# Gathers that leave item 0 out by a bounds check, in place of products that subtract it

## The chip, the cores and the metric

The kernel runs on one core of a Trainium2 chip, launched once with all its inputs in device memory. The metric is device time in microseconds (us). A time given for a kernel is the median of its runs; a profile is one more execution, in which the hardware profiler records each instruction, and that execution has a time of its own. Engines are called PE (TensorE, matrix products and transposes), DVE (VectorE), ACT (ScalarE), POOL (GpSimd) and SP (SyncE, which only issues transfers here).

## The reference

The inputs are a sequence of 50 item indices for each of 1024 users, a length per user, and a table of 100,001 items with 128 numbers each. Item 0 is a padding item: its row counts as zero, both where rows are gathered and in the product at the end.

```python
emb = emb_table.at[0].set(0.0)
e = emb[seq]                                   # 1024 x 50 x 128
prefix = jnp.cumsum(e, axis=1)
denom = jnp.minimum(t_idx[None, :], lengths[:, None])
uF = prefix / denom[:, :, None]
mean = uF.mean(axis=0)
var = uF.var(axis=0)
y = (uF - mean) * lax.rsqrt(var + BN_EPS) * gamma + beta
def step(v, x):                                # 50 steps
    v = v + (x - v) / TAU
    spike = atan_spike(v - V_TH)               # 1 where v >= V_TH
    v = v - spike * V_TH
    return (v, spike)
scores = spikes.mean(axis=0) @ emb.T           # 1024 x 100001
```

The scores are 1024 x 100,001 numbers of four bytes, 409.6 MB. The indices of the run are drawn evenly from 0 (in the first column from 159) up to between 90,260 and 99,965, so that an index 0 is rare: 1024 x 50 draws from some 100,000 values.

## The kernel before, in words

The kernel has two stages. In the first, a loop over the 50 steps t, the running sums are kept transposed, with the 128 features on the partitions and the 1024 users along the free axis, in two banks `pre[0]` and `pre[1]` of 512 users in PE's accumulator memory. In the second, the spike counts are multiplied with the whole table, and the scores are written out.

The order of the work is written out by hand (`tc.manual_schedule()`): each engine executes its instructions in the order in which the program names it, and only semaphores tie the engines together.

**The first stage.** `gather(t)` (L204) takes one of two buffers `e` (128 partitions x 1024 numbers, a pool with `bufs=2`) and has POOL issue eight indirect transfers (L207), one for each group of 128 users; each reads 128 indices from column t of the tile `idx` and fetches 128 rows of 512 bytes from the table. Gathers 0 and 1 are issued ahead of the loop; gather t + 2 is issued in step t, after PE has read buffer e_t. In step t PE transposes the eight blocks of e_t and adds them to `pre` (L324). DVE divides each half by the length into `uF` (L335) and takes its statistics (L336), which L342 joins to mean and variance. ACT takes a square root (L346) and subtracts the mean (L353); four small operations of DVE (L359 to L372) make the scale `a`; ACT applies it and writes the input x into the tile of v (L376, in the function `x`). DVE counts the spikes of the step before (L301), and adds the old state (L379, in `step`). ACT then computes v minus the threshold in bf16 (L294, in `over`), from which DVE makes the negative rest state in the next step (L298).

**Item 0.** The table as given does not have zeros in row 0, and the gathers fetch that row as it is. The kernel before subtracts it by products. At the start it makes `isz`, 1 where an index is 0 (L219 to L221), transposes it into `zT` (L224, L226), which has one row for each step and user, and splits row 0 of the table into a high and a low part, negated, in `r0n` (L227 to L232). `only(t)` (L267) builds, for five steps at a time, a matrix that is `r0n` where the row belongs to step t and zero elsewhere (L272), by means of `sel` (L234). `correct(t, l)` (L280) multiplies it with `zT` into both halves of `pre` (L282), which takes row 0 away from every user whose index is 0 in step t. Step t issues the correction of step t + 1, and the correction of step 0, with `start=True`, is what opens the accumulation. Row 0 of the table for the product at the end is set to zero separately (L133), which the change does not touch.

Beside the steps, SP fetches the first forty 1024-row blocks of the table (L109) at the start, and in steps 42 and 44 the first two are transposed (L136) and split into two parts for the product (L152 on ACT, L153 on DVE).

**The second stage** goes over 98 blocks of the table and eight groups of 128 users: products of both parts (L160), a scaled copy of the result by DVE or ACT (L512, L514), and the store of the scores (L169 on SP). The change does not touch it.

Of the kernel before, what the change touches and what calls it, by code (L numbers as in the profile page):

```python
# [12 lines left out]
F32 = mybir.dt.float32  # L13
BF16 = mybir.dt.bfloat16
F32R = mybir.dt.float32r
I32 = mybir.dt.int32
U32 = mybir.dt.uint32
AF = mybir.ActivationFunctionType
ALU = mybir.AluOpType

P = 128
# [4 lines left out]
BANK = 512  # L26
GROUP = 6
AHEAD = 6
ONLY = 5
TWICE = 2  # L30
ASIDE = 2
SHIFT = TWICE + ASIDE
# [7 lines left out]
def rec_kernel(  # L40
# [9 lines left out]
    nc = tc.nc  # L50
    B, T = seq.shape
    N, D = table.shape
    NB = B // P
# [21 lines left out]
    ident = const.tile([P, P], F32, tag="ident", name="ident")  # L75
# [11 lines left out]
    def pair(i):  # L87
        free.append([embp.tile([P, HALF], F32R, tag=f"{x}{i}", name=f"{x}_{i}") for x in ("hi", "lo")])
# [59 lines left out]
    def prepare(q, pt):  # L148
        turned(q, pt)
        split[q] = hi, lo = free.pop(0)  # L150
        vp, vh, vl = views(q, pt, hi, lo)
        nc.scalar.copy(vh, vp)  # L152
        nc.vector.tensor_tensor(vl, vp, vh.bitcast(F32), ALU.subtract)  # L153
# [18 lines left out]
    with ExitStack() as ph:  # L172
        once = ph.enter_context(tc.tile_pool(name="once", bufs=1))
        lp = ph.enter_context(tc.tile_pool(name="lif", bufs=1))
        sp = ph.enter_context(tc.tile_pool(name="stats", bufs=3))
        up = ph.enter_context(tc.tile_pool(name="uF", bufs=1))
        gp = ph.enter_context(tc.tile_pool(name="gather", bufs=2))
        accp = ph.enter_context(tc.tile_pool(name="acc", bufs=1, space=bass.MemoryType.PSUM))
        vp = ph.enter_context(tc.tile_pool(name="v", bufs=1, space=bass.MemoryType.PSUM))

        idx = once.tile([P, NB, T], I32, tag="idx", name="idx")
        nc.sync.dma_start(out=idx, in_=seq.rearrange("(p n) t -> p n t", n=NB))
        len_i = once.tile([P, NB], I32, tag="len_i", name="len_i")
        nc.sync.dma_start(out=len_i, in_=lengths.rearrange("(p n) -> p n", n=NB))
        r0 = once.tile([P, D], F32, tag="r0", name="r0")
        nc.sync.dma_start(out=r0, in_=table[0:1, :].to_broadcast([P, D]))
        gb = once.tile([P, 2], F32, tag="gb", name="gb")
        nc.sync.dma_start(out=gb[:, 0:1], in_=gamma.rearrange("(d o) -> d o", o=1))
        nc.sync.dma_start(out=gb[:, 1:2], in_=beta.rearrange("(d o) -> d o", o=1))
# [9 lines left out]

        es = {}

        def gather(t):  # L204
            es[t] = gp.tile([P, B], F32, tag="e", name=f"e_{t}")
            for n in range(NB):
                nc.gpsimd.indirect_dma_start(  # L207
                    out=es[t][:, n * P : (n + 1) * P],
                    out_offset=None,
                    in_=table,  # L210
                    in_offset=bass.IndirectOffsetOnAxis(ap=idx[:, n, t : t + 1].bitcast(U32), axis=0),
                )

        make_identity(nc, ident)
        isz = up.tile([P, NB, P], F32, tag="uF", name="isz")
        rb = up.tile([P, NB, P], F32, tag="uF", name="rb")
        gather(0)

        nc.vector.memset(isz, 0.0)  # L219
        for u in (0, P // 2):  # L220
            nc.vector.tensor_single_scalar(isz[:, :, u : u + T], idx, 0.0, ALU.is_equal)  # L221
        zps = vp.tile([P, B], F32, tag="v1", name="zps")
        for n in range(NB):
            nc.tensor.transpose(zps[:, n * P : (n + 1) * P], isz[:, n, :], ident)  # L224
        zT = once.tile([P, B], F32R, tag="zT", name="zT")
        nc.scalar.copy(zT, zps)  # L226
        r0hi = once.tile([P, D], F32R, tag="r0hi", name="r0hi")  # L227
        nc.scalar.copy(r0hi, r0)
        r0n = once.tile([P, D], F32, tag="r0n", name="r0n")
        nc.vector.tensor_scalar_mul(r0n, r0hi.bitcast(F32), -1.0)  # L230
        up2 = slice(P // 2, P)
        nc.vector.tensor_tensor(r0n[up2, :], r0hi[up2, :].bitcast(F32), r0[up2, :], ALU.subtract)  # L232
        sel = once.tile([P, P // 2], F32, tag="sel", name="sel")
        nc.vector.tensor_tensor(sel, ident[:, : P // 2], ident[:, P // 2 :], ALU.add)  # L234


        rl = once.tile([P, NB], F32, tag="rl", name="rl")
        nc.vector.tensor_copy(rl, len_i)
# [17 lines left out]
        count = once.tile([P, B], BF16, tag="count", name="count")  # L256
# [5 lines left out]

        pre = [accp.tile([P, BANK], F32, tag=f"pre{h}", name=f"pre{h}") for h in range(B // BANK)]

        ls = once.tile([P, ONLY, D], F32R, tag="ls", name="ls")

        def only(t):  # L267

            k = t % ONLY
            if k == 0:  # L270
                n = min(ONLY, T - t)
                nc.vector.tensor_tensor(  # L272
                    ls[:, :n, :],
                    r0n.unsqueeze(1).to_broadcast([P, n, D]),
                    sel[:, t : t + n].unsqueeze(2).to_broadcast([P, n, D]),
                    ALU.mult,
                )
            return ls[:, k, :]

        def correct(t, l):  # L280
            for h in range(B // BANK):
                nc.tensor.matmul(  # L282
                    pre[h],
                    lhsT=l,
                    rhs=zT[:, h * BANK : (h + 1) * BANK],
                    start=t == 0,
                    stop=False,
                    skip_group_check=True,
                )

        def over(t, v):

            d = lp.tile([P, B], BF16, tag="d", name=f"d_{t}")
            nc.scalar.activation(d, v, AF.Identity, bias=less)  # L294
            return d
# [4 lines left out]
        def spiked(out, cs, v):  # L300
            nc.vector.scalar_tensor_tensor(out, v, V_TH, count[:, cs], ALU.is_ge, ALU.add)  # L301
# [9 lines left out]

        v = None

        correct(0, only(0))
        l = only(1)
        gather(1)
        for t in range(T):
            last = t == T - 1
            e = es.pop(t)
            uF = up.tile([P, B], F32, tag="uF", name=f"uF_{t}")  # L320
            bs = sp.tile([P, B // BANK, 6], F32, tag="bs", name=f"bs_{t}")
            for h, cs in enumerate(halves):
                for k in range(0, BANK, P):
                    nc.tensor.matmul(  # L324
                        pre[h][:, k : k + P],
                        lhsT=e[:, h * BANK + k : h * BANK + k + P],
                        rhs=ident,
                        start=False,
                        stop=last,
                        is_transpose=True,  # L330
                        skip_group_check=True,
# [2 lines left out]
                        keep_busy(ident, KQ // 2)  # L334
                nc.vector.scalar_tensor_tensor(uF[:, cs], rlen[:, cs], 1.0 / (t + 1), pre[h], ALU.max, ALU.mult)  # L335
                nc.vector.bn_stats(bs[:, h, :], uF[:, cs])  # L336
            if t + 2 < T:
                gather(t + 2)
            if not last:
                correct(t + 1, l)  # L340
            mv = sp.tile([P, 2], F32, tag="mv", name=f"mv_{t}")
            nc.vector.bn_aggr(mv, bs.rearrange("p h s -> p (h s)"))  # L342

# [31 lines left out]
            def x(vt, cs):  # L375
                nc.scalar.activation(vt, uF[:, cs], AF.Identity, bias=hgb[:, 1:2], scale=a)  # L376

            def step(vt, cs):
                nc.vector.scalar_tensor_tensor(vt, negv[:, cs], -0.5, vt, ALU.mult, ALU.add)  # L379

            if not last:
                vt = vp.tile([P, B], F32, tag=f"v{(t + 1) % 2}", name=f"v_{t}")
                x(vt, whole)
                if t:
                    spiked(count, whole, v)
                step(vt, whole)
                v = vt
                if t == T - 2:
                    spiked(count, whole, v)
                    moved = once.tile([P, P], F32, tag="r0hi", name="moved")  # L390
                    nc.vector.tensor_scalar_add(moved, v[:, pieceA], beta2)
                    near = once.tile([P, P], F32, tag="r0", name="near")
                    nc.vector.scalar_tensor_tensor(near, v[:, pieceA], V_TH, moved, ALU.is_ge, ALU.subtract)
                d = over(t, v)
                if t + 2 < T:
                    l = only(t + 2)

                if t in (T - 8, T - 6):
                    q = (t - T + 8) // 2
                    pair(q)  # L400
                    prepare(q, vp.tile([P, HALF], F32, tag="v0", name=f"pt_{q}"))
                    if q == TWICE - 1:
                        for k in range(TWICE):
                            rows[GROUP + ASIDE + k] = first[:, k, :]
                        nc.sync.dma_start(
                            out=first[:, :TWICE, :],
                            in_=table[(GROUP + ASIDE) * HALF : (GROUP + SHIFT) * HALF, :].rearrange(
                                "(q p k) d -> p q (k d)", p=P, k=KQ
                            ),
                        )  # L410
# [53 lines left out]
    for c, W in enumerate(WIDTHS):  # L464
# [34 lines left out]
        for n in range(NB):  # L499
            if c == 0 and n == 0:  # L500
                continue
            pool, tag, most = turns[blocks % len(turns)]
# [23 lines left out]
            if n in (1, 4) and c >= MIDDLE and to_fetch < parts:  # L526
                g, k = divmod(to_fetch - SHIFT, GROUP)
# [26 lines left out]
```

## Time and profile before

| | |
|---|---|
| Time, median of 3 runs | 1573.99 us (1573.79 to 1574.6) |
| The profiled execution's own time | 1638.64 us |
| Its span, first to last instruction | 1636.8 us |
| Busy in the span: PE, DVE, ACT, POOL | 1085.8, 948.7, 673.0, 381.1 us |
| POOL's gathers: first and last start | 3.4 and 564.2 us |
| First store of scores issued | 577.6 us |
| Written to memory, read from memory | 409.6 MB, 77.7 MB |

A page of the profile has the busy time of each engine, the span in 40 equal slices of 40.9 us (a digit is the busy share of a slice in tenths), the queues of transfers, the chain of waits that ended last, and groups of instructions by source line. In a group's line stand the line, engine, operation, output and inputs with their shapes, the count, the busy time and the mean of one in ns, and the engine's idle time just before these instructions with what ended it. "issue" is time in which an engine waited for nothing that the profile shows; "remote" is a release whose source is not in the records.

### The profile page before, as it was taken

How to read it: one execution, taken by the hardware profiler on the slowest of the kernel's cores; microseconds unless marked ns; L12 is line 12 of the kernel's file. 1: busy time of each engine (PE TensorE's matmuls, PEld its weight loads, DVE VectorE, ACT ScalarE, POOL GpSimd, SP SyncE). 2: the span in 40 equal slices, each digit the busy share in tenths (PEclk: the TensorE clock that was granted, in tenths of full speed). 3: DMA queues.
4: the chain of work that ended last, by engine and by line, in shares of the span. 5: the costliest groups of instructions: out<-in, count | busy, mean ns of one | idle time of the engine just before them, and what ended most of it. 6: DMA issues, size and time to landing. Idle time of an engine off the chain costs nothing.

```text
span 1636.8 us, 12254 instructions
## 1 busy us (share of the span) xinstructions
PE 1085.8 (66%) x4464; PEld 806.9 (49%) x4464; DVE 948.7 (58%) x1127; ACT 673.0 (41%) x697; POOL 381.1 (23%) x406
## 2 busy tenths in 40 slices
PE   4333332333332488888988877888878888788884
PEld 2212111222112366666766666666666666566663
DVE  5666654677665865665755554555545555555652
ACT  2333322333323354555554444444444444444442
POOL 7666666766666500000000000000000000000000
PEclk7555555555555599999999999989999999999998
DMA  9611111111111279999999999999999999999998
GB/s 346 240 46 46 46 45 46 51 45 47 45 46 47 66 326 412 415 423 412 405 426 430 427 428 429 403 432 426 418 428 420 408 423 426 427 424 408 429 401 358
DMA packets 51313, 488.12 MB, mean 298 GB/s; under 512 B 10079, under 2 KB 10336, under 8 KB 30004
## 3 DMA queue, kind: packets, MB, share of 16 engines
q1 hardware_dynamic: 30752, 430.86, 62.6%
q0 software_dynamic: 12800, 26.24, 5.4%
q10 hardware_dynamic: 7700, 30.23, 4.5%
q8 instruction: 35, 0.57, 0.1%
q14 instruction: 26, 0.21, 0.0%
HBM read 77.69 MB, written 409.60 MB: 298 GB/s over the span
## 4 chain that ended last, share of the span: by engine, by line
DMA 42%; PE 16%; DVE 14%; another core or an unknown queue 9%; POOL 7%; issue 5%; ACT 5%; ACTq 0%; SPq 0%; DVEq 0%; POOLq 0%
DMA scores<-o 40%; PE po L160 14%; POOL e L207 7%; DVE o L512 3%; ACT o L514 3%; DVE uF L335 2%; DVE bs L336 2%; DMA e<-in_L_rec_emb_table,idx 2%; DVE v L379 2%; DVE negv L298 1%; ACT v L376 1%; PE pre L324 1%; DVE count L301 1%; DVE pairs L153 1%
## 5 line engine op out<-in xcount | busy, mean ns | idle before, releaser
L512 DVE TENSOR_SCALAR o<-po 128x1024 f32<-128x1024 f32 (+1 forms) x391 | 467.4, 1214 | 326.0 <-DMA scores<-o 183.8
L514 ACT ACTIVATE o<-po 128x1024 f32<-128x1024 f32 x391 | 391.8, 1025 | 503.9 <-DMA scores<-o 358.6
L207 POOL DMA_INDIRECT e<-in_L_rec_emb_table,idx x400 | 380.4, 951 | 183.5 <-issue 110.9
L160 PE MATMUL po<-pairs,countB 128*128 128x512 f32 (+1 forms) x1120 | 291.2, 406 | 61.1 <-ACT o L514 61.1
L160 PE MATMUL po<-pairs,countC 128*128 128x512 f32 (+1 forms) x840 | 237.8, 430 | 59.0 <-ACT o L514 53.1
L160 PEld LDWEIGHTS po<-pairs,countB 128*128 128x128 f32 x1120 | 210.4, 193 | 122.0 <-ACT o L514 80.0
L282 PE MATMUL pre<-zT,ls 128*128 128x512 f32 x100 | 78.4, 786 | 271.2 <-DVE uF L335 227.2
L160 PEld LDWEIGHTS po<-pairs,countC 128*128 128x128 f32 x840 | 166.2, 205 | 111.0 <-ACT o L514 65.0
L282 PEld LDWEIGHTS pre<-zT,ls 128*128 128x128 f32 x100 | 29.0, 291 | 309.9 <-DVE uF L335 255.7
L324 PE MATMUL pre<-ident,e 128*128 128x128 f32 x400 | 126.8, 435 | 79.5 <-DMA e<-in_L_rec_emb_table,idx 63.0
L335 DVE SCALAR_TENSOR_TENSOR uF<-rlen,pre 128x512 f32<-128x512 f32 x100 | 68.0, 680 | 161.7 <-remote 124.4
L324 PEld LDWEIGHTS pre<-ident,e 128*128 128x128 f32 x400 | 80.4, 209 | 126.8 <-DMA e<-in_L_rec_emb_table,idx 94.7
L153 DVE TENSOR_TENSOR pairs<-pt,pairs 128x1024 fp32r<-128x1024 f32 x70 | 85.3, 1218 | 96.1 <-ACT pairs L152 96.0
L346 ACT ACTIVATE r<-mv,eps 128x1 f32<-128x1 f32 x50 | 14.8, 295 | 273.0 <-DVE mv L342 181.0
L136 PE MATMUL pt<-ident,rows 128*128 128x128 f32 (+1 forms) x768 | 105.6, 283 | 9.9 <-issue 4.9
L136 PEld LDWEIGHTS pt<-ident,rows 128*128 128x128 f32 (+1 forms) x768 | 95.1, 148 | 27.4 <-issue 11.5
L160 PE MATMUL po<-hi,countB 128*128 128x512 f32 x208 | 85.4, 411 | 13.9 <-ACT o L514 13.6
L152 ACT CAST pairs<-pt 128x1024 fp32r<-128x1024 f32 x70 | 70.1, 1013 | 41.0 <-PE pt L136 41.0
L160 PE MATMUL po<-lo,countB 128*128 128x512 f32 x208 | 83.2, 400 | 0.0
L294 ACT ACTIVATE d<-v,less 128x1024 bf16<-128x1024 f32 x49 | 54.5, 1113 | 65.4 <-DVE v L379 36.3
L160 PE MATMUL po<-hi,countC 128*128 128x512 f32 x156 | 66.5, 426 | 14.2 <-ACT o L514 12.6
L376 ACT ACTIVATE v<-uF,hgb,a 128x1024 f32<-128x1024 f32 x49 | 59.2, 1208 | 31.0 <-DVE a L372 11.7
(88 smaller groups left out, 887.2 us busy)
## 6 DMA issues: line engine op xcount, KB each, us to landing
scores<-o SPq DMA_DIRECT2D x96, 3072.0 KB
scores<-o SPq DMA_DIRECT2D x32, 1536.0 KB
scores<-o SPq DMA_DIRECT2D x30, 1024.0 KB
rows<-in_L_rec_emb_table ACTq DMA_DIRECT2D x19, 1536.0 KB
scores<-o SPq DMA_DIRECT2D x8, 2896.5 KB
rows<-in_L_rec_emb_table SPq DMA_DIRECT2D x5, 3072.0 KB
e<-in_L_rec_emb_table,idx POOLq DMA_INDIRECT x400
rows<-in_L_rec_emb_table SPq DMA_DIRECT2D x2, 1024.0 KB
```

The costliest lines, as they stand in the source:

```text
L136: nc.tensor.transpose(pt[:, k0 : k0 + pw], r[:pw, k0 : k0 + D], ident[:pw, :pw])
L152: nc.scalar.copy(vh, vp)
L153: nc.vector.tensor_tensor(vl, vp, vh.bitcast(F32), ALU.subtract)
L160: nc.tensor.matmul(po[:, :kw], lhsT=counts[n], rhs=part[:, k0 : k0 + kw], start=j == 0, stop=j == 1,)
L207: nc.gpsimd.indirect_dma_start(out=es[t][:, n * P : (n + 1) * P], out_offset=None, in_=table, in_offset=bass.IndirectOffsetOnAxis(ap=idx[: ...
L282: nc.tensor.matmul(pre[h], lhsT=l, rhs=zT[:, h * BANK : (h + 1) * BANK], start=t == 0, stop=False, skip_group_check=True,)
L294: nc.scalar.activation(d, v, AF.Identity, bias=less)
L324: nc.tensor.matmul(pre[h][:, k : k + P], lhsT=e[:, h * BANK + k : h * BANK + k + P], rhs=ident, start=False, stop=last, is_transpose=True, ...
L335: nc.vector.scalar_tensor_tensor(uF[:, cs], rlen[:, cs], 1.0 / (t + 1), pre[h], ALU.max, ALU.mult)
L376: nc.scalar.activation(vt, uF[:, cs], AF.Identity, bias=hgb[:, 1:2], scale=a)
L512: nc.vector.tensor_scalar_mul(o[:, h0 : h0 + hw], po[:, :hw], 1.0 / T)
L514: nc.scalar.mul(o[:, h0 : h0 + hw], po[:, :hw], 1.0 / T)
```

## The change

The products for item 0 are taken out, with all that prepares them: `isz`, `zT`, `r0hi`, `r0n`, `sel`, `ls`, `only`, `correct` and the load of row 0. In their place, the indices themselves are changed at the start: `away` sets an index 0 to N = 100,001, one past the last row, for column 0 first and then for the other 49. The indirect transfers get a bounds check against N - 1, with which an index beyond the table is left out and its 128 numbers of the buffer keep what they held. So each buffer is cleared before it is gathered into: `clear` has ACT copy a column of zeros, broadcast, over the 128 x 1024 buffer.

The accumulation is now opened by two products of zeros (the tile `count`, zero at that point) with `start=True`. The place of `gather(t + 2)` within a step changes as well: it was issued right after the statistics of step t, and is now issued after ACT's x (L376 of before), so that its clear stands between L376 and L294 on ACT, and the eight gathers wait for that clear.

```diff
-        r0 = once.tile([P, D], F32, tag="r0", name="r0")
-        nc.sync.dma_start(out=r0, in_=table[0:1, :].to_broadcast([P, D]))
...
+        none = once.tile([P, NB, T], I32, tag="none", name="none")
+
+        def away(ts):
+            nc.vector.tensor_scalar(none[:, :, ts], idx[:, :, ts], 0.0, float(N), ALU.is_equal, ALU.mult)
+            nc.vector.tensor_tensor(idx[:, :, ts], idx[:, :, ts], none[:, :, ts], ALU.max)
+
+        away(slice(0, 1))
+        away(slice(1, T))
+        nil = once.tile([P, 1], F32, tag="nil", name="nil")
+        nc.vector.memset(nil, 0.0)
+
+        def clear(e):
+            nc.scalar.activation(e, nil.to_broadcast([P, B]), AF.Copy)
+
         es = {}
 
         def gather(t):
             es[t] = gp.tile([P, B], F32, tag="e", name=f"e_{t}")
+            clear(es[t])
             for n in range(NB):
                 nc.gpsimd.indirect_dma_start(
                     out=es[t][:, n * P : (n + 1) * P],
                     out_offset=None,
                     in_=table,
                     in_offset=bass.IndirectOffsetOnAxis(ap=idx[:, n, t : t + 1].bitcast(U32), axis=0),
+                    bounds_check=N - 1,
+                    oob_is_err=False,
                 )
...
-        nc.vector.memset(isz, 0.0)
-        for u in (0, P // 2):
-            nc.vector.tensor_single_scalar(isz[:, :, u : u + T], idx, 0.0, ALU.is_equal)
...
-        correct(0, only(0))
-        l = only(1)
+        for h in range(B // BANK):
+            nc.tensor.matmul(
+                pre[h],
+                lhsT=count[:, :P],
+                rhs=count[:, h * BANK : (h + 1) * BANK],
+                start=True,
+                stop=False,
+                skip_group_check=True,
+            )
         gather(1)
...
-            if t + 2 < T:
-                gather(t + 2)
-            if not last:
-                correct(t + 1, l)
             mv = sp.tile([P, 2], F32, tag="mv", name=f"mv_{t}")
...
                 x(vt, whole)
+                if t + 2 < T:
+                    gather(t + 2)
                 if t:
                     spiked(count, whole, v)
                 step(vt, whole)
...
                 d = over(t, v)
-                if t + 2 < T:
-                    l = only(t + 2)
-
```

More of the change, by code (lines that the diff above doesn't have):

```diff
@@ L28 @@
 AHEAD = 6
-ONLY = 5
 TWICE = 2
@@ L211, in gather @@
                     in_offset=bass.IndirectOffsetOnAxis(ap=idx[:, n, t : t + 1].bitcast(U32), axis=0),
+                    bounds_check=N - 1,
+                    oob_is_err=False,
                 )
         make_identity(nc, ident)
-        isz = up.tile([P, NB, P], F32, tag="uF", name="isz")
         rb = up.tile([P, NB, P], F32, tag="uF", name="rb")
         gather(0)
-        nc.vector.memset(isz, 0.0)
-        for u in (0, P // 2):
[L221 to L234, printed above, removed]
         rl = once.tile([P, NB], F32, tag="rl", name="rl")
@@ L263, in rec_kernel @@
         pre = [accp.tile([P, BANK], F32, tag=f"pre{h}", name=f"pre{h}") for h in range(B // BANK)]
[L265 to L289, printed above, removed]
         def over(t, v):
```

## The prediction, made before the changed kernel had run

> **What bounds the kernel now.** I read the page's forty slices first, for the stages.
>
> ```profile
> PE   4333332333332488888988877888878888788884
> DVE  5666654677665865665755554555545555555652
> ACT  2333322333323354555554444444444444444442
> POOL 7666666766666500000000000000000000000000
> DMA  9611111111111279999999999999999999999998
> ```
>
> A slice is 40.9 us. For fourteen slices GpSimd (POOL) works while PE, ACT and the DMA engines are mostly idle; then POOL stops and the DMA engines are full. The change touches the first stage alone. Next I read the groups:
>
> ```profile
> L207 POOL DMA_INDIRECT e<-in_L_rec_emb_table,idx x400 | 380.4, 951 | 183.5 <-issue 110.9
> ...
> L282 PE MATMUL pre<-zT,ls 128*128 128x512 f32 x100 | 78.4, 786 | 271.2 <-DVE uF L335 227.2
> ```
>
> The 400 gathers of L207, eight a step, take 951 ns each and follow one another after about 0.30 us ("issue"). The L282 products, which go, keep PE busy for 78.4 us, but PE waits 271.2 us ahead of them. The timeline of one undisturbed step says who is late; columns are start and duration in us:
>
> ```profile
> 203.66 0.94 POOL L207 DMA_INDIRECT e<-in_L_rec_emb_table,idx  x1 [0.30 <-issue]
> 204.91 0.94 POOL L207 DMA_INDIRECT e<-in_L_rec_emb_table,idx  x1 [0.30 <-issue]
> ...
> 206.15 0.47 PE L324 MATMUL pre<-ident,e 128*128 128x128 f32 x1 [0.75 <-DMA e<-in_L_rec_emb_table,idx]
> ...
> 206.83 0.67 DVE L335 SCALAR_TENSOR_TENSOR uF<-rlen,pre 128x512 f32<-128x512 f32 x1
> ...
> 210.48 1.21 ACT L376 ACTIVATE v<-uF,hgb,a 128x1024 f32<-128x1024 f32 x1 [0.64 <-issue]
> ...
> 211.72 1.23 DVE L379 SCALAR_TENSOR_TENSOR v<-negv,v 128x1024 f32<-128x1024 f32 x1 [0.20 <-ACT v L376]
> ...
> 212.98 1.11 ACT L294 ACTIVATE d<-v,less 128x1024 bf16<-128x1024 f32 x1 [1.30 <-DVE v L379]
> ...
> 214.89 0.94 POOL L207 DMA_INDIRECT e<-in_L_rec_emb_table,idx  x1 [0.30 <-issue]
> ```
>
> The gather of 203.66 is the eighth of a step t, that of 204.91 the first for t+1, that of 214.89 the first for t+2. POOL's beat is thus (214.89 - 204.91)/8 = 1.248 us, 9.98 us a step, and PE waits for each landing. DVE's own share of a step (two L335, two L336, L342, L298, the four small ones, L301, L379) sums to 7.4 us. POOL bounds the stage.
>
> The waits of the first stage (40 to 560 us; total, times, longest) show what disturbs the beat:
>
> ```profile
> DVE uF L335 <- remote: 124.4, 18, 10.0
> ...
> POOL e L207 <- remote: 50.0, 10, 5.8
> ...
> POOL e L207 <- PE pre L282: 13.7, 3, 5.4
> ```
>
> Some PE results reach DVE up to 10 us late, from a cause that the profile doesn't name, and POOL then waits 13 times, 63.7 us in all. The profiled execution took 1638.64 us (span 1636.8 and 1.8 around it), the median is 1573.99: 64.65 us less. The two agree so well that I take these stalls to belong to the profiled execution alone, and the unprofiled first stage to be POOL's beat from first gather to last.
>
> **What the Trainium skill says.** Four places.
> - "Perfetto Trace Analysis", DMA Instruction — SWDGE: such a gather's profiled end is the end of descriptor generation, not of the transfer; GpSimd instructions are to be timed start to start. The trace agrees: 0.94 us end before the data do (204.91's gather lands after 2.46 us by the chain), so the price is 1.248.
> - "Advanced Engine Details and Errata", Sequencer Loop: a sequencer reads ahead and queues engine instructions while others run. The trace agrees for POOL: its 48 semaphore instructions of 17 ns on L207's queue leave the beat at 1.25 (241.56 to 242.81 with one between).
> - "ScalarE: Activation LUTs", What ACT_TABLE_LOAD costs: an ACTIVATE with immediate scale and bias takes 186 ns + 0.833 N. For N = 1024 an estimate of 1.04 us; L514, a copy of 128x1024, measures 1025 ns. That page's Table sets section has copy in every set; the built program has no more table loads than before.
> - "GPSIMD Engine Reference", 3.1: a compare and select costs 1.03 to 2.03 cycles, data-dependent branching some 12 cycles an element, at 1.2 GHz. No run here shows a checked gather.
>
> **The change, part by part.**
>
> *Products gone* (100 of L282, 10 of L272, the set-up for item 0): 78.4 us of PE and 8.1 us of DVE, all while PE waits for landings and DVE has 9.98 - 7.4 = 2.6 us a step free. Worth 0, as POOL still sets the step.
>
> *Clears* (50 on ACT, 1.04 us each, 52 us of ACT). 48 stand behind L376 and ahead of L294. ACT is free from 211.69; the clear would run to 212.73, and L294 can't start before L379 ends at 212.95. So nothing on ACT moves: 0. Without that cover each would delay L294 by up to 1.04 us, and DVE's L298 of the next step, which has a few microseconds.
>
> *The moved gather.* Eight gathers and their clear now come after L376 of step t, where before they waited only for PE's transposes of e_t. On ACT, the clear's own waits (eight landings and PE) are over before L376 runs; queued behind it are L294 and the next step's L346. On POOL only gathers queue, in the same order; the first of eight now waits for ACT. It could start at about 212.8 and is due at 214.89: 2.1 us are left, so 0. In the two steps with an extra split (t = 42 and 44), DVE's L153 of 1.2 us pushes the next step's L335 by 0.9 us at most; 1.2 us are left. The margin was 214.89 - 206.62 = 8.3 us. That matters only where PE is late: a stall that POOL meets would cost up to 8.3 - 2.1 = 6.2 us more, in the profiled execution.
>
> *Start-up.* The first gather now waits for index work, a memset and a clear:
>
> ```profile
> 3.23 0.65 DVE L221 TENSOR_SCALAR isz<-idx 128x400 f32<-128x400 int32 x2 [1.29 <-DMA idx<-in_r_seq]
> 3.40 1.16 POOL L207 DMA_INDIRECT e<-in_L_rec_emb_table,idx  x1 [2.09 <-DMA idx<-in_r_seq]
> ```
>
> From 3.23: two operations on 128x8 (0.25 each, as L239 to L240: 0.31), one like L221 on 128x392 (0.37), a two-operand one on 392 columns (0.5: L272 needs 0.76 for 640), the memset, clear's start: 4.75. Plus 1.04 and a hand-over: 5.95 instead of 3.40, +2.55 us, between 1.9 and 3.3. All of POOL's beat moves with it, and nothing behind absorbs it: the last landing releases the last step. The second gather's long 2.32 us at 13.61 may recur or not: up to -1.4.
>
> *The bounds check*, 400 times on the bounding engine. In the built program each gather gets a register move ahead of it for the bound. The trace has one such move on POOL, 35 ns; hidden by reading ahead: 0, in series: 400 x 0.035 = 14 us. Then the descriptor loop itself. It works 128 indices in 0.944 us, 8.9 cycles each at the page's clock. Bounds: below, nothing or slightly less than nothing, if the check is always made or has a loop of its own; above, 12 cycles of branch x 128 = 1.28 us a gather, 512 us. Between: a vector compare of some 16 cycles, 13 ns, 5 us; one cycle per descriptor, 107 ns, 43 us. I take 0, since a loop that must build an address per index can hold the compare where it has slack; this is the least certain step. Nothing is skipped: indices are drawn from some 100,000 items, 51,200 draws, half an item 0 expected, so transfers stay as they are.
>
> Sum in the profiled execution, stalls apart: 2.55. Unprofiled: 1573.99 + 2.55 = 1576.5 us.
>
> **Rivals.**
> 1. *Forecast*: check free, start-up paid. 1576.5, from 1574.5 to 1579.
> 2. *Small price per gather*: the register move in series or a vector compare, 13 to 35 ns: 5 to 14 us more, 1582 to 1591. For it: one more instruction per gather on the bounding engine. Against: the semaphore instructions that cost nothing.
> 3. *The check in the descriptor loop* (the other side). Place: inside L207; price 43 us a cycle: 1576.5 + 43 = 1619 for one, 1662 for two, 2088 for a branch. It decides from 1.5 ns a gather, where 2.55 + 400 x 0.0015 passes 0.2%. For it: nothing hides POOL. Against: nothing in the trace.
> 4. *The stalls are no matter of the profiler.* Then the margin lost costs 13 x 6.2 = 81 us: 1657. Against: 64.65 and 63.7 agree.
> 5. *Faster*: POOL's waits for L282 (13.7 us) exist unprofiled and go with the products, or the checked loop is shorter: 1573.99 + 2.55 - 13.7 = 1562.8. Against: as 4.
>
> **How the numbers follow.** 0.2% is 3.1 us, about what a measurement of this kernel can tell from no change. Chances: forecast 55, of which 40 within 0.2% and 15 just over; rival 2, 18; rival 3, 14; rival 4, 5; rival 5, 8. Faster 0.08, same 0.40, slower 0.52. The range reaches from 1574 to 1622: it leaves out rival 5 below (8), rival 4 and the half of rival 3 above one cycle (12).
>
> **What would show it.** In the changed profile: L207's successor start to start at 1.248 us (rivals 2 and 3: longer, and by how much); the first gather near 6 us; clears of about 1.04 us between the x activation and the threshold, which starts when it did; POOL "issue" 0.30. If stalls come as often, POOL's waits grow from 64 us to some 145, and the profiled span to about 1720 us though the median hardly moves. A beat that is off by 10 ns, or a median that follows the profiled span, makes the prediction wrong.

## The result and the profile after

The changed kernel takes 1597.1 us, median of four runs (1595.87 to 1597.89), beside 1573.89 us for the kernel before: a ratio of 1.0148 (95% interval 1.0135 to 1.0161), 23.2 us more. The time lies within the predicted range, 20.6 us above the predicted value. Its profiled execution took 1596.43 us (span 1594.6).

From the page, the slices (39.9 us each here) of PE, GpSimd, PE's granted clock and the transfers:

```profile
PE   3333333333333799889988788888888788888884
POOL 6777777777777100000000000000000000000000
PEclk9999999999985799999998998999989999899998
DMA  9611111111112599999999999999999999999998
```

The picture is that of before: for 13 slices GpSimd works at six to seven tenths while PE stands at three and, after the first two slices, the transfers stand at one; then the transfers are full. The stage is still GpSimd's. Its groups, from the same page:

```profile
L219 POOL DMA_INDIRECT e<-in_L_rec_emb_table,idx x400 | 398.7, 997 | 127.5 <-issue 108.5
L300 PE MATMUL pre<-ident,e 128*128 128x128 f32 x400 | 183.1, 466 | 319.2 <-DMA e<-in_L_rec_emb_table,idx 293.6
```

L219 is L207 of before: 400 gathers again, but 997 ns each where the median was 944 (the mean of 951 in the page of before holds a few long ones). PE (L300, before L324) still waits for landings. One step of the timeline (start and duration in us):

```profile
205.13 1.00 POOL L219 DMA_INDIRECT e<-in_L_rec_emb_table,idx  x1 [0.30 <-issue]
...
210.56 1.21 ACT L348 ACTIVATE v<-uF,hgb,a 128x1024 f32<-128x1024 f32 x1 [0.63 <-DVE a L344]
...
211.70 1.04 ACT L211 ACTIVATE e<-nil 128x1024 f32<-128x1024 f32 x1
211.80 1.23 DVE L351 SCALAR_TENSOR_TENSOR v<-negv,v 128x1024 f32<-128x1024 f32 x1 [0.20 <-ACT v L348]
...
213.06 1.11 ACT L263 ACTIVATE d<-v,less 128x1024 bf16<-128x1024 f32 x1 [0.32 <-DVE v L351]
...
215.54 0.99 POOL L219 DMA_INDIRECT e<-in_L_rec_emb_table,idx  x1 [0.30 <-issue]
```

The first gathers of two steps start at 205.13 and 215.54, so the beat is (215.54 - 205.13)/8 = 1.301 us, before 1.248. The gap ("issue") is 0.30 us as before: the gather itself has grown. The clear (L211) takes 1.04 us and ends at 212.74, and L263 (L294 of before) starts at 213.06, as soon as L351 has ended at 213.03. The first gather of the next step, for which the clear makes room, is due only at 215.54: 2.8 us of margin. The start of the kernel, in the same view:

```profile
3.32 0.17 DVE L202 TENSOR_SCALAR none<-idx 128x8 int32<-128x8 int32 x1 [3.32 <-DMA idx<-in_r_seq]
...
4.00 0.57 DVE L203 TENSOR_TENSOR idx<-idx,none 128x392 int32<-128x392 int32 x1
...
4.52 0.06 DVE L208 MEMSET nil<- 128x1 f32 x1
4.63 2.00 ACT L211 ACTIVATE e<-nil 128x1024 f32<-128x1024 f32 x2 [2.61 <-DVE nil L208]
...
5.97 1.14 POOL L219 DMA_INDIRECT e<-in_L_rec_emb_table,idx  x1 [4.66 <-ACT e L211]
```

The first gather starts at 5.97 us, before 3.40. GpSimd's waits (total, times, longest) and then the records of the gather's line, its register moves among them:

```profile
POOL e L219 <- issue: 108.5, 356, 0.3
POOL e L219 <- DMA e<-in_L_rec_emb_table,idx: 11.9, 39, 0.3
POOL e L219 <- ACT e L211: 7.1, 5, 4.7
```

```profile
L219 POOLq MOVE  x400: 29/29/29, 1.0 to 517.9; - x134
L219 POOL DMA_INDIRECT e<-in_L_rec_emb_table,idx x400: 992/997/1139, 6.0 to 526.5; - x134
```

GpSimd waits for a clear five times: 4.66 us at the start, and 2.4 us in four waits, all in the first 60 us, while the bulk rows of the table are still being loaded; 0.30 us stands ahead of every gather anyway, so these four cost 1.2 us. No "remote" wait is left. The sum: 399 x (1.301 - 1.249) = 20.7 us for the gathers, with the median beat of either trace, and 2.57 for the start, 23.3 us against 23.2 measured. It leaves out terms of one to two microseconds that nearly cancel, such as these waits and what the products cost (below).

### The profile page after: what moved, and what is told of

It is laid out like the page before. It is cut to its first block, busy times and chain, and to the rows that moved or that the text cites. A ratio compares the mean times of both kernels' runs of the same rounds, so it can differ in the third digit from the quotient of the medians.

```text
span 1594.6 us, 12766 instructions
## 1 busy us (share of the span) xinstructions
PE 1082.3 (68%) x4358; PEld 781.4 (49%) x4358; DVE 941.6 (59%) x1116; ACT 720.8 (45%) x745; POOL 399.3 (25%) x406
## 4 chain that ended last, share of the span: by engine, by line
DMA 49%; POOL 15%; PE 14%; issue 12%; DVE 5%; ACT 4%; POOLq 0%; ACTq 0%; SPq 0%; DVEq 0%
DMA scores<-o 43%; POOL e L219 15%; PE po L159 13%; DMA e<-in_L_rec_emb_table,idx 6%; DVE o L483 3%; ACT o L485 3%; DVE pairs L152 1%; ACT pairs L151 1%; POOLq L219 0%; PE pt L135 0%; ACT hi L151 0%; DVE lo L152 0%; DMA idx<-in_r_seq 0%; ACT third L151 0%; ACTq L485 0%
## 5 line engine op out<-in xcount | busy, mean ns | idle before, releaser
L219 POOL DMA_INDIRECT e<-in_L_rec_emb_table,idx x400 | 398.7, 997 | 127.5 <-issue 108.5
L300 PE MATMUL pre<-ident,e 128*128 128x128 f32 x400 | 183.1, 466 | 319.2 <-DMA e<-in_L_rec_emb_table,idx 293.6
L300 PEld LDWEIGHTS pre<-ident,e 128*128 128x128 f32 x400 | 73.1, 184 | 429.6 <-DMA e<-in_L_rec_emb_table,idx 318.2
L159 PE MATMUL po<-pairs,countC 128*128 128x512 f32 (+1 forms) x840 | 241.2, 435 | 57.3 <-ACT o L485 50.5
L159 PEld LDWEIGHTS po<-pairs,countC 128*128 128x128 f32 x840 | 169.4, 209 | 109.9 <-ACT o L485 62.6
L312 DVE BATCH_NORM_STATS2 bs<-uF 128x6 f32<-128x512 f32 x100 | 69.4, 694 | 3.4
L159 PE MATMUL po<-pairs,countA 128*128 128x512 f32 x280 | 68.3, 393 | 4.0 <-ACT o L485 3.4
L351 DVE SCALAR_TENSOR_TENSOR v<-negv,v 128x1024 f32<-128x1024 f32 x49 | 60.3, 1230 | 11.4 <-ACT v L348 11.4
```

The source lines that it names most:

```text
L159: nc.tensor.matmul(po[:, :kw], lhsT=counts[n], rhs=part[:, k0 : k0 + kw], start=j == 0, stop=j == 1,)
L219: nc.gpsimd.indirect_dma_start(out=es[t][:, n * P : (n + 1) * P], out_offset=None, in_=table, in_offset=bass.IndirectOffsetOnAxis(ap=idx[: ...
L300: nc.tensor.matmul(pre[h][:, k : k + P], lhsT=e[:, h * BANK + k : h * BANK + k + P], rhs=ident, start=False, stop=last, is_transpose=True, ...
```

## The experiments

The theory: the check costs some 53 ns inside each gather, the start 2.6 us, everything else next to nothing. Rivals: the register move ahead of each gather costs the time; the clears or the moved gather do. For the stalls that the profile of before showed, the rival is that they are no matter of profiling.

### Which part costs

These four ran on one chip, where the kernel before took 1574.75 us. The first leaves the check out of the changed kernel (an index 0 still becomes N, and without the check would fetch the row past the table's end, so item 0 isn't left out); the second puts it alone into the kernel before.

```diff
-                    bounds_check=N - 1,
-                    oob_is_err=False,
```

> The changed kernel with the bounds check alone taken out of its gathers (an index 0 would read past the table; none is drawn, so the output stays). Theory: the check sits in the gather's descriptor loop. Then the beat of the gathers goes back from 1.300 to 1.248 us start to start, and the time to 1573.9 + 2.6 of start-up = 1576.5 us. Rival (the clears, or the gathers that now wait for ACT, hold the beat): the beat stays near 1.30 and the time near 1597 us.

> The kernel before with the bounds check alone added to its gathers; products, places and buffers as before, indices unchanged. Theory: 400 x 0.053 us = 21 us more, 1595 us, gathers of 997 ns with gaps of 0.305. Rival: 1574 us. Beside it the profile shows PE's clock with the products in: if it is the products that lower PE's clock and make PE's results late, the first stage shows the clock near 0.5 and waits of POOL as in the profile before; if that belonged to one execution, the clock is near 1 and POOL doesn't wait.

Measured: 1578.2 without the check (ratio 1.0022, 1.0014 to 1.003), 1594.82 with the check alone (1.0126, 1.0111 to 1.0142). The groups of their pages, first without, then with:

```profile
L219 POOL DMA_INDIRECT e<-in_L_rec_emb_table,idx x400 | 378.3, 946 | 129.6 <-issue 118.0
```

```profile
L207 POOL DMA_INDIRECT e<-in_L_rec_emb_table,idx x400 | 400.4, 1001 | 123.9 <-issue 114.9
```

The gather's duration goes with the check and with nothing else: 946 ns in the changed program without it, 1001 in the old program with it. Put into the old program the check costs 20.1 us (1594.82 - 1574.75); all the rest of the change costs 3.4 (1578.2 - 1574.75). Together they are 23.5 us, beside 23.2 for the change. Taken out of the changed program it saves 18.8 us (1596.97 in the next run, with the check, less 1578.2). That rules out clears and moved gather as the main cost.

The third loads the bound once into a register, so that the 400 moves are gone.

```diff
+        top = nc.gpsimd.to_reg(N - 1)
...
-                    bounds_check=N - 1,
+                    bounds_check=top,
```

> The changed kernel with the bound loaded into one register once, so that the 400 register moves on POOL's queue are gone and the check stays. Theory: the price is in the loop and the moves (29 ns each) are read ahead while a gather runs: no change, 1597 us, beat 1.300. Rival (the moves stand in series): 400 x 0.029 = 12 us less, 1585 us.

Measured: 1596.97 (1.014, 1.0124 to 1.0156), with a beat of 1.301 and this group:

```profile
L220 POOL DMA_INDIRECT e<-in_L_rec_emb_table,idx x400 | 398.6, 996 | 127.4 <-issue 110.0
```

Taking the 400 moves of 29 ns away saves nothing that shows (12 us was the rival's figure). The rival of the register move falls, and the price sits inside the gather.

The fourth takes the products of steps 1 to 49 out of the kernel before (item 0 isn't subtracted in those steps).

```diff
-            if not last:
-                correct(t + 1, l)
...
-                if t + 2 < T:
-                    l = only(t + 2)
```

> The kernel before with the products for item 0 of steps 1 to 49 taken out, and nothing put in their place (item 0 is not subtracted in these steps; that part of the work is left out). Theory: POOL's beat sets the stage and the products are covered: 1573.9 us, unchanged. Rival (they hold POOL up by PE being late): up to 13.7 us less, 1560 us. In the profile: PE's clock in the first stage near 1 if the products are what lowers it.

Measured: 1573.0 (0.9989, 0.9983 to 0.9996), beat 1.251. The products of these 49 steps are worth 1.75 us, 0.6 to 2.7 by the interval; where those lie, no trace shows. In this profiled execution GpSimd met no "remote" wait, as in the three above, and each of the four spans is 1.4 to 2.6 us under its kernel's median: profiling as such adds no 64 us. Since this trace has no stalls, that of the changed kernel can be laid beside it: its first gather comes 2.4 us later (5.97 and 3.54), first to last gather take 20.0 us more (520.5 and 500.5), and what follows 0.6 us more.

### Where the stalls come from

The next four ran on another chip, where the kernel before takes 1636.16 us (1634.66 to 1641.04, nine runs). One of them is the kernel before, unchanged.

> The kernel before once more, for a second profile. Theory: PE's clock of 0.5 and the late PE results belong to the one execution first profiled: this profile shows a clock near 1 in the first stage, no waits of POOL, and a span near 1572 us, as the kernel with the check alone did with all the products in. Rival (the profiler brings them in this kernel): 1637 us again.

Measured: 1635.21. The slices of PE's clock, and waits of GpSimd and DVE:

```profile
PEclk9999999999999599999999999899999999899998
```

```profile
POOL e L207 <- remote: 56.6, 13, 5.6
```

```profile
DVE uF L335 <- remote: 116.0, 17, 10.0
```

The stalls are those of the first profile of before (63.7 us in 13 waits there), at a clock of nine tenths or more in the first stage, where that profile had mostly five tenths. On this chip the nine runs of the kernel before had a mean clock of 0.79 to 0.80 (five) or 0.96 (four) and took 1636 us at either (medians 1636.16 and 1635.59); on the first chip its runs at 0.81 took 1574 to 1575. So neither one odd execution nor a low clock makes them, and the profiler by itself doesn't, since the four profiles above have none.

The traces with stalls have one more thing in common. The page's list of transfers ends with the median time from issue to landing, where the landings were recorded; of before, then of the changed kernel:

```profile
e<-in_L_rec_emb_table,idx POOLq DMA_INDIRECT x400
```

```profile
e<-in_L_rec_emb_table,idx POOLq DMA_INDIRECT x400, 2.5
```

The figure is missing in the profile that the prediction read and in all four on this chip, and stands (2.4 to 2.6) in every other trace. A gather leaves 16 records when it lands, 6400 in all; the changed kernel's trace has 6400, that of before 1183, that of before again 1253. In these two the records thin out between two stalls and come back just after each. So the profile that the prediction read, at 1638.64 us, is like those of this chip, and the three times beside it are like those of a chip without stalls.

As far as three chips can tell, the stalls go with the chip. Two things stay open. Each chip was used in one sitting, so chip and sitting aren't told apart. And each run listed for these experiments comes with a clock and a span, so something was recorded in all of them: whether this chip makes PE late by itself, or only while it is being recorded, no run shows.

The next experiment is the changed kernel with the marking of 49 columns of indices put behind the first gathers and the memset ahead of all; the one after it clears each buffer five times.

```diff
+        nil = once.tile([P, 1], F32, tag="nil", name="nil")
+        nc.vector.memset(nil, 0.0)
...
         away(slice(0, 1))
-        away(slice(1, T))
-        nil = once.tile([P, 1], F32, tag="nil", name="nil")
-        nc.vector.memset(nil, 0.0)
...
         gather(0)
+        away(slice(1, T))
```

> The changed kernel with its start put in another order: the zero column first, then column 0 of the indices, and the other 49 columns only behind the first gather. Theory: the first gather waits for the index load and two operations on 128x8 (0.2 us each) and starts at 4.0 us instead of 5.97, the clear being done by then; all of POOL's beat moves, so 2 us less than the changed kernel: 1595 us. Rival (the start is absorbed later): 1597 us.

```diff
-            nc.scalar.activation(e, nil.to_broadcast([P, B]), AF.Copy)
+            for _ in range(5):
+                nc.scalar.activation(e, nil.to_broadcast([P, B]), AF.Copy)
```

> The changed kernel with each buffer cleared five times over. Theory: the clear ends 2.8 us before POOL needs it, so the first 2.8 us of the four further clears (4 x about 1.0 us) are free and the rest, 1.2 us, holds up every other gather in effect: about 0.6 us a step, 29 us, 1626 us; POOL then waits for ACT in most steps. Rival (the clears cost in full at their place): 48 x 4 us = 190 us more. Rival (they are free whatever their number): 1597 us.

Measured: 1679.25 (ratio 1.0245, 1.0223 to 1.0267) for the early gather, 1658.3 (1.0131, 1.0113 to 1.015) for five clears. GpSimd's waits for the clear with the early gather, and the gathers of before again and of the early gather, with the first and last start in us:

```profile
POOL e L218 <- ACT e L210: 72.3, 12, 10.2
```

```profile
L207 POOL DMA_INDIRECT e<-in_L_rec_emb_table,idx x400: 938/944/2327, 3.6 to 562.0; - x134
L218 POOL DMA_INDIRECT e<-in_L_rec_emb_table,idx x400: 993/1000/1140, 4.6 to 600.7; - x134
```

On this chip the order of the changed kernel loses 43.1 us to the kernel before, not 23.2. In the two traces the stretch from first to last gather is 596.1 us, before 558.4: of those 37.6 us, 399 x (1.304 - 1.249) = 21.9 are the longer beat and the remaining 15.7 are longer waits; the first gather is 1.0 us later, and 5.4 more pass after the last one. Where a PE stall of some 10 us cost GpSimd about 5 in the kernel before (5258, 5062, 5023 ns over the beat), it now costs up to 9.9 (9887, 9877), since the buffer's clear waits in ACT's queue behind work that needs the late result. The margin that the change gave up is real, but only a chip with stalls charges for it. The first gather came at 4.62 us, not at 4.0 as expected.

Five clears are 21 us faster than the early gather because their trace has no late PE result: no "remote" wait is in it. Why the stalls stay away there is open (of the 6400 landing records it has 2616), but it shows that the chip alone doesn't bring them. Without stalls the trace can be laid beside the changed kernel's of the first section here, and the spans differ by 62.1 us (1656.7 and 1594.6): the first gather comes 4.2 us later (10.17), first to last gather take 57.9 more (578.4 and 520.5), the rest the same. The waits stand right behind the clears:

```profile
330.13 5.39 ACT L212 ACTIVATE e<-nil 128x1024 f32<-128x1024 f32 x5
...
335.79 1.00 POOL L220 DMA_INDIRECT e<-in_L_rec_emb_table,idx  x1 [1.80 <-issue]
```

The clears end at 335.52 and the gather follows at 335.79, 1.5 us past its beat; in the middle of the stage two steps lose some 1.9 us together. The expectation had 1.2 us in two steps and 29 us in all: its mechanism came, and its size was half of what was measured. So clears are free only inside the margin of 2.8 us, and cost time beyond it.

In the last of the four, half of all indices (those under 50,000) are set to N in the changed kernel, so that half of the rows are left out.

```diff
-            nc.vector.tensor_scalar(none[:, :, ts], idx[:, :, ts], 0.0, float(N), ALU.is_equal, ALU.mult)
+            nc.vector.tensor_scalar(none[:, :, ts], idx[:, :, ts], 50000.0, float(N), ALU.is_lt, ALU.mult)
```

> The changed kernel with every index below 50,000 set to N instead of the index 0 alone, so that about half of all rows are left out (the scores then lack these items). Theory: the check costs its 53 ns on every gather, whatever it finds, and a row that is left out still passes through the loop: beat 1.30 us or a little less, 1597 us. Rival (a row left out leaves the loop early, or saves its descriptor): gathers clearly shorter than 0.94 us, 1550 us or less. Rival (leaving out is the slow branch): gathers longer than 1.0 us.

Measured: 1682.8, one run; moved bytes fell from 488.1 to 475.0 MB, some 25,600 rows of 512 bytes. The records of the gather's line:

```profile
L219 POOL DMA_INDIRECT e<-in_L_rec_emb_table,idx x400: 991/997/1139, 6.0 to 602.7; - x134
```

The chip's stalls are in this time too. The gather is as long when half of its rows are out of bounds as when none is: 997 ns. A left-out row saves its transfer and none of GpSimd's time.

### A third chip: what the price goes by

On a third chip the kernel before takes 1574.31 us. The changed kernel once more, and with the early gather:

> The changed kernel as it is, once more, beside the kernel before on the same chip. Theory: the check costs 53 ns a gather, 400 gathers 21 us, and the start 2.6 us; on a chip where the kernel before takes 1574 us this gives 1597, a ratio of 1.014 to 1.015. On a chip where the kernel before takes about 1636 us because TensorE's results reach VectorE late, the cleared tile is also late behind those stalls and GpSimd waits for it: 1670 to 1685, a ratio of 1.02 to 1.03. Rival: the stalls cost both kernels the same, and the difference is 23 us on either chip.

> The changed kernel with the bound's marking of 49 of the 50 columns moved behind the first step's gathers, so that the first gather waits for the memset of one column, the marking of one column and the clear alone. The first gather at 4.6 us as seen in the other run of this kernel, in place of 5.97, so 1.3 us less than the changed kernel of the same call where GpSimd's chain sets the end. Rival: the start is absorbed by the waits of the first 60 us (some 2.4 us in four waits), and the time is the changed kernel's to 0.3 us.

Measured: 1597.69 (ratio 1.0148, 1.0131 to 1.0165) and 1595.74 (1.0139, 1.0122 to 1.0156). The first repeats the result. The start of the second, with DVE's marking of the other 49 columns ahead of the first gather:

```profile
3.98 0.57 DVE L203 TENSOR_TENSOR idx<-idx,none 128x392 int32<-128x392 int32 x1
...
4.59 1.14 POOL L218 DMA_INDIRECT e<-in_L_rec_emb_table,idx  x1 [3.28 <-DVE idx L203]
```

The gather starts at 4.59, 1.38 us ahead of the 5.97 above, and although this marking was placed behind it, it starts only after that has ended (4.55). The median fell by 1.95 us, which agrees with 1.3, but the two intervals overlap: not settled.

The last two are the kernel before with gathers of 64 rows, without and with the check; both leave out half of the users' rows.

```diff
+            if t < 2:
+                nc.vector.memset(es[t], 0.0)
...
-                    out=es[t][:, n * P : (n + 1) * P],
+                    out=es[t][: P // 2, n * P : (n + 1) * P],
...
-                    in_offset=bass.IndirectOffsetOnAxis(ap=idx[:, n, t : t + 1].bitcast(U32), axis=0),
+                    in_offset=bass.IndirectOffsetOnAxis(ap=idx[: P // 2, n, t : t + 1].bitcast(U32), axis=0),
```

> The kernel before with gathers of 64 rows in place of 128: the other half of the users' rows is left out (their parts of the two first tiles are zero). No check. If a gather's time goes by rows, about 470 to 500 ns each; if half of it is fixed, about 700 ns. It is the base for the run after it.

> The same with the bounds check in the gathers; half of the users' rows are left out here too. If the check is paid per row, a gather is 26 ns longer than without it in the run before; if it is paid once per gather, 53 ns longer.

Measured: 1560.31 and 1574.96 us, one run each. Their groups, without and with:

```profile
L209 POOL DMA_INDIRECT e<-in_L_rec_emb_table,idx x400 | 362.7, 907 | 126.8 <-issue 112.4
```

```profile
L209 POOL DMA_INDIRECT e<-in_L_rec_emb_table,idx x400 | 378.7, 947 | 126.7 <-issue 109.4
```

Neither expectation held. Half the rows make the gather 39 ns shorter (946 to 907), 0.6 ns a row: nearly all of its duration is a price per instruction. The check costs 40 ns at 64 rows and about 52 at 128, so half the rows save less than a quarter of it. Through two points, an estimate: 28 ns a gather and 0.19 ns a row. It is rough, since medians of the same gather differ by 3 ns from one execution to another (944 and 947, 997 and 1000).

## Why the prediction was right in part

- **The bound** was read rightly: GpSimd's chain sets the first stage before and after, and a longer gather came through to the end in full (20.7 us of longer beat, 20.1 us of time).
- **The bounds check** is the step that failed: "I take 0, since a loop that must build an address per index can hold the compare where it has slack". It costs 52 ns a gather, so this term of the sum is 20.7 us, not 0. By the prediction's own sign, a beat that is off by 10 ns, its account fails here. Both parts of the reason fell: there was no slack, and the loop's price is not one per index. The 8.9 cycles an index came from dividing the whole duration by 128; by the 64-row gathers an index takes 0.6 ns of it. The Trainium skill has this in "DMA: Bandwidth & Descriptors", Anatomy of one DMA: many descriptors can be issued before their number shows in the cost. The traces agree (64 rows fewer, 39 ns less), and the prediction didn't draw on it. And the price lies between its cases: more than rival 2's 35 ns, in rival 3's place, at half of its one cycle per index. The 12 cycles a branch from "GPSIMD Engine Reference", 3.1, would have been 1.28 us a gather; nothing of that size was seen. (The figures for a compare and select that the prediction places in 3.1 stand in section 7 of that page, "Performance pitfalls for Q7 kernels".)
- **The register move** at nothing was right: 400 moves of 29 ns, and 1596.97 us without them.
- **The start-up** was right: 5.95 predicted, 5.97 measured, +2.57 for +2.55.
- **The clears** were right: 1038 ns for 1.04, and L263 starts with the end of L351, as L294 did after L379. Five clears pass the margin and are paid for.
- **The moved gather** was right in the steady steps, with 2.8 us of margin for 2.1. It missed the first 60 us, where four waits cost 1.2 us.
- **The products** at 0 were right within the bound of 0.2% (3.1 us): 1.75 us measured. Rival 5 falls: the kernel before with the check alone still has all products, and its trace has no wait of GpSimd for them.
- **The stalls**: "The two agree so well that I take these stalls to belong to the profiled execution alone" led to the right base for a reason that the runs don't bear out. All nine runs of one chip carry the stalls' time, and the median there lies 61.4 us above the first chip's (1636.16 and 1574.75), while profiled executions on the other chips have none. If it is the chip, the right base was luck in where the medians were taken. Rival 4's mechanism holds on a chip with stalls, but there both kernels carry them: 4.6 us more for the longest waits (5.3 to 9.9) where it had 6.2, and 15.7 us of waits over the stage where it had 81, in part because stalls came once in some six steps in place of four to five.

The range held by its width, 48 us (1574 to 1622): it reached to the middle case of an unknown price on the bounding engine. The predicted value took that price at its lower end for no reason that a row of the profile gave.

## What to carry to other kernels

An option on an instruction that is repeated on the bounding engine is priced at more than nothing until a trace shows it: 50 ns, 400 times, were nearly the whole result, while 52 us of new ACT work and 78 us of removed PE work moved it by two or three us. Before a duration is divided by its elements, vary the size: here half the rows took 96% of the time. Cover has an end: one clear fits into 2.8 us of margin, five cost 62 us. And when a profiled execution differs from the medians, ask first whether it ran on the same chip and whether its records are complete.

## What the runs showed of the hardware

- An indirect gather of 128 rows of 512 bytes occupies GpSimd for 944 to 947 ns (medians), one of 64 rows for 907; another starts 0.30 us later. The bounds check adds some 52 and 40 ns. Rows out of bounds save nothing of it.
- One chip of those used runs the same kernel in 1636 us where two others take 1574. On it PE's results reach DVE up to 10 us late, with PE's clock at nine tenths or more. In the kernel before such stalls came once in four to five steps (some 45 to 50 us), one or two together; in the changed order once in six (some 73 us), mostly three close together; with five clears not at all. So the spacing follows the program and not the time alone. Most landing records are lost in the traces from there. What the stalls are, the profile doesn't name, and whether they come without recording, no run shows.
